# Layer 0's last tile in a two-layer graph network: GpSimd's additions behind VectorE's pieces, and two TensorE steps of the next stage a place earlier

## The chip, the cores and the metric

The kernel runs on one core of a Trainium2 chip. Its engines are TensorE (PE in the profile; its weight loads are shown as PEld), VectorE (DVE), ScalarE (ACT), GpSimd (POOL) and SyncE (SP), which issues most of the loads. The metric is the device time of one execution in microseconds (us), as the median of several runs. One further execution was taken by the hardware profiler; all times inside the kernel are from that one, counted from the start of its span.

## What is computed

Eight batches of 2048 nodes with 64 channels pass through two graph layers. Each adds its output to its input and normalises every node over its 64 channels.

```python
# layer 0: w = embedding x weight (D = 16, K = 3), per node
As = [eye(N), A, 2.0 * (A @ A) - eye(N)]
x_g = einsum('knm,bmc->bnkc', stack(As), x)
out = einsum('bnki,nkio->bno', x_g, w) + b
x = layernorm(x + out)
# layer 1: both supports are the same adj
out = concat([x, A x, 2 A A x - x, A x, 2 A A x - x]) @ weight + bias
x = layernorm(x + out)
```

The adjacency matrix is sparse, its rows are scaled by one number each, and the kernel works with its pattern of zeros and ones.

## The kernel before

The work is cut into 16 tiles of 128 nodes. The stages follow one another in program order: two hops of layer 0 (products with the 2048 x 2048 pattern); for each tile the mixing with the per-node weights (`mix0`), its norm and the projection for layer 1; then two hops of layer 1 and the output. TensorE is busy nearly throughout.

**Order.** Instructions that go through `ordered` (L127) stay in program order on their engine. So each of VectorE, ScalarE and GpSimd has one strict queue, and an instruction that waits holds back all behind it. SyncE's loads are in program order too (L123). Waits for data and buffers are put in by the framework, which also decides which of a ring's buffers a new tile gets.

**The pieces of a tile.** `mix0` (L402) has eight pieces, each a product into its own pair of PSUM banks; there are four pairs. A piece is (g, i): g is the half of the batches, 0 or 1. With i under 2, ScalarE scales the piece by the node's embedding and puts it aside in two SBUF tiles (L423, tiles `aside` of the ring `raw`, which has five buffers). With i of 2 or more, VectorE adds it into the sum `acc` by four instructions (L433). `add_aside(g)` then lets GpSimd add the aside tiles together, in three instructions, and the result into half g of `acc` by a fourth (all L441). The list `at[n]` says what is put into the program ahead of piece n.

**The norm.** `layernorm` (L359) is a generator. Its first part reduces `acc` (L362, L363, VectorE) and subtracts the mean on GpSimd (L365), giving `xc`; n1 squares on ScalarE (L353); n2 sums the squares (L370, VectorE) and takes the root (L372, ScalarE); n3 takes the reciprocal (L374, VectorE) and finishes with six GpSimd instructions (L375 to L380), the last of which multiplies `xc`. During tile t the norm of tile t-1 is finished.

**The last tile, 15.** Its `at` lists (L874 to L880) hold, besides n1 to n3 of tile 14's norm, the calls `early(i, ...)`: parts of step i of the next stage, namely the high part (ScalarE, L234) and low part (VectorE, L238) of the operand y, the load of S (L123) and its cast (ScalarE, L646). Steps 0 and 1 get all of them early, steps 2 to 4 only y. The pieces of the last tile are (0,0), (0,1), (0,4), (1,0), (0,5), (1,1), (1,4), (1,5).

**The next stage.** `third` is layer 1's first hop as seven products of eight steps each (`seven_products`, L580). A step is eight matmuls (L658). Its load of S has the lead 4, its cast of S the lead 2: they stand that many steps ahead in the program. S is loaded into the ring `raw`, where the aside tiles are, too. Its accumulators take over the four pairs of PSUM banks. In the first product the accumulators of the second, `sums3[1]`, are free, and there the last two tiles are finished: `last_transposed` transposes `xc` (eight on TensorE, L300, and ScalarE's copy hT, L306), `last_projected` projects it (sixteen matmuls, L460, and six ScalarE copies to z, L469). For tile 14 these come after steps 1 and 2, for tile 15 after steps 6 and 7 (L830 to L833). The norm of tile 15 is finished by three calls in the list `todo` (L892), of which two entries are taken after each step: n1 and n2 after step 2, n3 after step 3.

Of the kernel before, what the change touches and what calls it, by code (L numbers as in the profile page):

```python
# [14 lines left out]
ALU = mybir.AluOpType  # L15
# [5 lines left out]
NT = N // P  # L21
# [18 lines left out]
def pattern(  # L40
# [22 lines left out]
    nc = tc.nc  # L63

    def pool(stack, name, bufs, **kw):
        return stack.enter_context(tc.tile_pool(name=name, bufs=bufs, **kw))
# [17 lines left out]
    def bank(name):  # L84

        return psum.tile([P, 2, 512], F32, tag="ps", name=name)
# [20 lines left out]
    part = keep.tile([P, B], F32, tag="part", name="part")  # L107
# [19 lines left out]
    def ordered(ins):  # L127
        if in_order:
            tc.keep_in_program_order(ins)
# [28 lines left out]
    def keep_node_bias(pb, h):  # L158
        to = ebias[:, 8 * h : 8 * h + 8, :].rearrange("p (g t) c -> p g (t c)", g=2)
        ordered(nc.vector.tensor_copy(to, pb[h][:, :, : 4 * C]))  # L160
# [198 lines left out]
    def layernorm(src):  # L359

        s = work.tile([P, B], F32, tag="ln_s", name="s")
        ordered(nc.vector.tensor_reduce(s, src, AX.X, ALU.add))  # L362
        ordered(nc.vector.tensor_tensor(s, s, part, ALU.mult))  # L363
        xc = xcpool.tile([P, B, C], F32, tag="ln_xc", name="xc")
        ordered(nc.gpsimd.tensor_tensor(xc, src, wide(s), ALU.subtract))  # L365
        yield xc.rearrange("p b c -> p (b c)")
        sq = squares(xc)
        yield
        ss = work.tile([P, B], F32, tag="ln_ss", name="ss")
        ordered(nc.vector.tensor_reduce(ss, sq, AX.X, ALU.add))  # L370
        sd, r0, va, q, r = [work.tile([P, B], F32, tag=f"{name}{B}", name=name) for name in ("ln_sd", "ln_r0", "ln_v", "ln_q", "ln_r")]
        ordered(nc.scalar.activation(sd, ss, AF.Sqrt, bias=eps, scale=1.0 / C))  # L372
        yield
        ordered(nc.vector.reciprocal(r0, sd))  # L374
        ordered(nc.gpsimd.tensor_scalar(va, ss, -0.5 / C, -0.5 * EPS, ALU.mult, ALU.add))  # L375
        ordered(nc.gpsimd.tensor_tensor(q, r0, r0, ALU.mult))
        ordered(nc.gpsimd.tensor_tensor(q, q, va, ALU.mult))
        ordered(nc.gpsimd.tensor_scalar(q, q, 1.0, 1.5, ALU.mult, ALU.add))
        ordered(nc.gpsimd.tensor_tensor(r, q, r0, ALU.mult))
        ordered(nc.gpsimd.tensor_tensor(xc, xc, wide(r), ALU.mult))  # L380
        yield
# [20 lines left out]
    def mix0(t, tt, acc, at, pieces):  # L402

        def block(pm, lhsT, ds):
            for k in range(3):
                for n in range(3):
                    for j in range(2):
                        q = slice(j * C, (j + 1) * C)
                        nc.tensor.matmul(  # L409
                            pm[:, j], lhsT=tt[k][n][q, lhsT, :], rhs=w_parts[n][k][q, ds, :],  # L410
                            start=(k == 0 and n == 0), stop=(k == 2 and n == 2),
                        )

        def e(d):
            return emb_sb[:, t, d : d + 1]

        def by_batch(g, i):
            pm = bank("pm").rearrange("p j (d c) -> p j d c", c=C)
            block(pm, 2 * g + i, slice(0, 2 * DG))
            if i == 0:  # L420
                aside[g] = [rawp.tile([P, DG, 2, 2, C], F32, tag="raw", name="aside") for _ in range(2)]
            for d in range(2 * DG):
                ordered(nc.scalar.activation(aside[g][d // DG][:, d % DG, :, i, :], pm[:, :, d, :], AF.Copy, scale=e(d)))  # L423

        def by_four(g, dg):
            dg -= 2
            pm = bank("pm").rearrange("p j (i d c) -> p j i d c", i=2, d=DG)
            for i in range(2):
                block(pm[:, :, i], 2 * g + i, slice(dg * DG, (dg + 1) * DG))
            for d in range(DG):  # L430
                part = acc[:, 4 * g : 4 * g + 4, :]
                got = pm[:, :, :, d, :].rearrange("p j i c -> p (j i) c")
                ordered(nc.vector.scalar_tensor_tensor(part, got, e(dg * DG + d), part, ALU.mult, ALU.add))  # L433

        aside = {}

        def add_aside(g):
            one, other = [a.rearrange("p d j i c -> p d (j i) c") for a in aside[g]]
            part = acc[:, 4 * g : 4 * g + 4, :]
            for to, more in ((one, other), (one[:, :2], one[:, 2:]), (one[:, 0], one[:, 1]), (part, one[:, 0])):  # L440
                ordered(nc.gpsimd.tensor_tensor(to, to, more, ALU.add))  # L441

        for n, (g, i) in enumerate(pieces):
            for work_here in at[n]:
                if isinstance(work_here, int):
                    add_aside(work_here)
                else:
                    work_here()
            (by_batch if i < 2 else by_four)(g, i)
        return layernorm(acc)  # L450

    def project(t, hT, pus=None):
# [260 lines left out]
    pieces = chain(weights(), weight_parts())  # L713
# [38 lines left out]
    def piece():  # L752
        ordered(next(pieces))

    more = {
        (0, 3): [
            lambda: node_bias(sums2[1]),
            lambda: todo.extend(lambda h=h: keep_node_bias(sums2[1], h) for h in range(2)),
        ],
        1: [piece] * 11,  # L760
        (2, 0): [lambda: load_weights(0, 2)],
        (3, 0): [lambda: load_weights(1)],
        2: [piece] * 8,
# [21 lines left out]
    def last_transposed(t):  # L785
        last_h["T"] = transpose(last_h[t], "hT", sums3[1][0])

    def last_projected(t):
        project(t, last_h["T"], (sums3[1][1], sums3[1][0]))
        if t < NT - 1:  # L790
            return
        layer0.close()
        t_pool = pool(tpool, "fzT", 1, reuse_waits="tile")
        for a in range(2):
            for c in range(2):
                zT[a, c] = t_pool.tile([P, 4, B * C], F32, tag=f"zT{a}{c}", name="zT")
# [22 lines left out]
    def quarter_back(a, b, which):  # L819
# [9 lines left out]
    third = seven_products(0, to_zT, sums3, {  # L829
        (0, 1): [lambda: last_transposed(NT - 2)],  # L830
        (0, 2): [lambda: last_projected(NT - 2)],
        (0, 6): [lambda: last_transposed(NT - 1)],
        (0, 7): [lambda: last_projected(NT - 1)],  # L833
        **{(2 + t // KK, t % KK): [lambda t=t: add_bias(t)] for t in range(NT)},
        3: quarter_back(1, 1, 1), 4: quarter_back(0, 1, 0), 5: quarter_back(0, 0, 1),
    }, wait=2)
# [3 lines left out]
    def early(i, *kinds):  # L840

        got = third_got.setdefault(i, {})
        for lead, part in sorted(third[i], key=lambda part: -part[0]):
            if part.__name__ in kinds:
                part(got)
        third[i] = [part for part in third[i] if part[1].__name__ not in kinds]
# [4 lines left out]
    y, s = ("y_high", "y_low"), ("load_sum", "operands")  # L851
    acc, h, norm = first_tile[5], None, None
    tt = first_tile[0]
    coming = operands(1)
    for t in range(NT):
        got, last = {}, t == NT - 1
        at = [[] for _ in range(8)]
        n1, n2, n3 = [lambda: next(norm)] * 3 if t else [nothing] * 3

        if not last:  # L860
            following, of_x, of_hop, of_second = coming
            of_hop = of_hop()
            at[1] += [go(of_x)] * (1 if t else 3)
            at[2] += [go(of_hop), n1, go(of_hop), go(of_hop), n2]
            if t + 2 < NT:
                at[2] += [lambda: times_r(t + 2)]
                at[4] += [lambda: got.update(coming=operands(t + 2))]
            at[3] += [n3, go(of_second), lambda: got.update(acc=begin_sum(t + 1))]
            at[4] += [go(of_second), go(of_second)]
            at[6] += [0]  # L870
            at[7] += [lambda: got.update(hT=transpose(h, "hT"))] if t else []
            pieces = [(0, 0), (0, 4), (0, 5), (1, 2), (0, 1), (1, 3), (1, 4), (1, 5)]
        else:
            at[1] += [n1, lambda: early(0, *y, *s)]  # L874
            at[2] += [n2, n3, lambda: early(1, *y, *s)]
            at[3] += [0, lambda: early(2, *y)]
            at[4] += [lambda: early(3, *y)]
            at[5] += [lambda: early(4, *y)]
            at[7] += [1]
            pieces = [(0, 0), (0, 1), (0, 4), (1, 0), (0, 5), (1, 1), (1, 4), (1, 5)]  # L880
        norm_now = mix0(t, tt, acc, at, pieces)
        if 0 < t < NT - 1:
            project(t - 1, got["hT"])
        if "coming" in got:
            coming = got["coming"]
            next(coming[1])
            next(coming[1])
        norm = norm_now
        last_h[t] = h = next(norm)
        if not last:  # L890
            tt, acc = following, got["acc"]
# [480 lines left out]
```

## Time and profile before

| | |
|---|---|
| median of 3 runs | 765.86 us (765.76 to 765.98) |
| the profiled execution, whole | 768.08 us |
| its span in the profile | 766.3 us |
| mean granted clock of TensorE | 0.996 |
| busy: VectorE, ScalarE, GpSimd | 559.4, 407.1, 270.0 us |
| tile 15's pieces on TensorE | 508.67 to 525.86 us |
| first matmul of the next stage | 527.91 us |
| first matmul of its second product | 549.60 us |

Every line of a profile names the source line, the engine, the operation, and output and inputs by the program's names. A wait is written as who waited, an arrow, and who released it, followed by the sum, the number and the longest. The chain of work that ended last is followed back from the last instruction of the run, at each step to whatever released it. The table of stretches gives busy time and number of instructions for each engine, then the clock that TensorE was granted (1.00 is full speed), the DMA share and GB/s. "x4" after an operation means four instructions merged into one row, with the time from the first's start to the last's end.

### The profile page before, as it was taken

Reading aid. Unit: us, or ns where it says so; the run is one execution under the profiler, and the core shown is the slowest. Engines: PE = TensorE matmul, PEld = TensorE weight load, DVE = VectorE, ACT = ScalarE, POOL = GpSimd, SP = SyncE. Lnnn points to the kernel's source line nnn. Section 1 sums busy time; section 2 is a strip of 40 time slices with the busy share of each in tenths; the row PEclk is TensorE's granted clock in tenths of the full one; section 3 lists DMA queues with packets and bytes.
Section 4 is the critical chain, followed back from the end, with each engine's and each line's share of the span. In section 5 each row is a group of like instructions: output and inputs, shape, how many; then the busy total and the mean of one; then the engine's idle time right before and its main releaser. Section 6 shows DMA issues by size and latency. Waiting matters only on the chain.

```text
span 766.3 us, 16926 instructions
## 1 busy us (share of the span) xinstructions
PE 755.8 (99%) x6634; PEld 661.4 (86%) x6634; DVE 559.4 (73%) x1159; ACT 407.1 (53%) x896; POOL 270.0 (35%) x297
## 2 busy tenths in 40 slices
PE   9999999999999999999999999998999999999996
PEld 6888888888889999999999999997788888888885
DVE  6768867678748888888888888866588648668663
ACT  5456533878755555555555555565887663112111
POOL 0000000000026788777778888867100000011341
PEclk9999999999999999999999999999999999999999
DMA  9998996555511000000000000003354444565631
GB/s 323 371 388 269 348 317 212 173 169 160 171 56 31 16 16 15 17 16 15 17 16 16 15 17 2 2 30 97 104 168 142 137 152 137 176 182 171 212 126 45
DMA packets 73558, 96.69 MB, mean 126 GB/s; under 512 B 4864, under 2 KB 48384, under 8 KB 73344
## 3 DMA queue, kind: packets, MB, share of 16 engines
q1 hardware_dynamic: 62064, 76.66, 31.5%
q10 hardware_dynamic: 11408, 18.89, 6.6%
q8 instruction: 54, 0.88, 0.5%
q14 instruction: 32, 0.26, 0.1%
HBM read 76.65 MB, written 18.87 MB: 125 GB/s over the span
## 4 chain that ended last, share of the span: by engine, by line
PE 96%; ACT 2%; POOL 1%; DVE 1%; issue 0%; POOLq 0%; DVEq 0%
PE pm L409 34%; PE accT L658 27%; PE acc L254 15%; PE a L254 10%; PE accT L254 6%; PE pu L460 2%; PE pt L300 1%; PE first L143 1%; PE accT L810 1%; POOL aside L441 1%; ACT aside L423 1%; ACT z L469 0%; DVE acc L433 0%; ACT s L646 0%; PE accT L460 0%
## 5 line engine op out<-in xcount | busy, mean ns | idle before, releaser
L433 DVE SCALAR_TENSOR_TENSOR acc<-pm,pack_sb,acc 128x256 f32<-128x256 f32 x376 | 181.0, 482 | 43.8 <-PE pm L409 28.1
L658 PE MATMUL accT<-s,hl 128*128 128x512 f32 x896 | 208.1, 393 | 2.6 <-DVE acc L433 2.1
L409 PE MATMUL pm<-wh,hl 64*128 64x512 f32 (+1 forms) x1332 | 207.8, 303 | 0.0
L409 PE MATMUL pm<-wm,parts 64*128 64x512 f32 (+1 forms) x1332 | 203.4, 296 | 0.0
L409 PE MATMUL pm<-wl,parts 64*128 64x512 f32 (+1 forms) x1332 | 203.3, 296 | 0.0
L658 PEld LDWEIGHTS accT<-s,hl 128*128 128x128 f32 x896 | 168.4, 189 | 39.1 <-issue 2.5
L409 PEld LDWEIGHTS pm<-wh,hl 64*128 64x128 f32 x1332 | 130.8, 187 | 4.0 <-issue 0.4
L409 PEld LDWEIGHTS pm<-wl,parts 64*128 64x128 f32 x1332 | 130.7, 187 | 3.7
L409 PEld LDWEIGHTS pm<-wm,parts 64*128 64x128 f32 x1332 | 130.4, 187 | 3.8
L646 ACT CAST s<-raw 128x1024 fp32r<-128x1024 bf16 x104 | 109.8, 1056 | 40.7 <-ACT hl L234 23.8
L254 PE MATMUL acc<-hl,s 128*128 128x512 f32 x512 | 116.5, 390 | 0.0
L254 PEld LDWEIGHTS acc<-hl,s 128*128 128x128 f32 x512 | 96.0, 188 | 20.4 <-issue 0.3
L423 ACT ACTIVATE aside<-pm,pack_sb 128x128 f32<-128x128 f32 x272 | 74.2, 389 | 48.1 <-PE pm L409 48.1
L709 POOL TENSOR_TENSOR z<-z,rrow 128x512 f32<-128x512 f32 x16 | 21.0, 1314 | 212.1 <-DVE z L682 212.1
L234 ACT CAST hl<-z 128x256 fp32r<-128x256 f32 (+1 forms) x96 | 47.8, 517 | 59.7 <-PE acc L254 22.9
L441 POOL TENSOR_TENSOR aside<-aside 128x1024 f32<-128x1024 f32 (+2 forms) x51 | 75.4, 1478 | 2.7
L254 PE MATMUL a<-hl,s 128*128 128x512 f32 (+1 forms) x352 | 73.4, 370 | 0.0
L254 PEld LDWEIGHTS a<-hl,s 128*128 128x128 f32 x352 | 61.9, 188 | 11.3
L320 POOL TENSOR_TENSOR parts<-parts 128x512 fp32r<-128x512 f32 x45 | 58.4, 1298 | 34.9 <-DVE parts L314 27.4
L238 DVE TENSOR_TENSOR hl<-z,hl 128x512 fp32r<-128x512 f32 (+1 forms) x96 | 54.0, 568 | 16.8 <-ACT hl L234 13.8
L287 POOL TENSOR_TENSOR z<-z,got 128x512 f32<-128x512 f32 x3 | 4.8, 1622 | 142.6 <-ACT got L286 142.6
L254 PE MATMUL accT<-hl,s 128*128 128x512 f32 x192 | 44.3, 390 | 0.0
(136 smaller groups left out, 814.1 us busy)
## 6 DMA issues: line engine op xcount, KB each, us to landing
raw<-in_adj SPq DMA_DIRECT2D x58, 512.0 KB, 5.8
raw<-sums_of SPq DMA_DIRECT2D x64, 256.0 KB, 2.8
sums_of<-z ACTq DMA_DIRECT2D x16, 512.0 KB, 6.7
raw<-quarters SPq DMA_DIRECT2D x32, 256.0 KB, 2.7
raw<-in_adj SPq DMA_DIRECT2D x16, 384.0 KB, 3.4
quarters<-seen ACTq DMA_DIRECT2D x16, 256.0 KB, 6.2
xt<-in_xT SPq DMA_DIRECT2D x16, 256.0 KB, 2.7
z<-in_x SPq DMA_DIRECT2D x15, 256.0 KB, 6.9
```

Source lines behind the costliest of these rows:

```text
L234: ordered(nc.scalar.copy(to[0], src))
L238: ordered(nc.vector.tensor_tensor(to[1], src, to[0], ALU.subtract))
L254: nc.tensor.matmul(accs[i], lhsT=s[:, i * P : (i + 1) * P], rhs=hl[h], start=(first and h == 0), stop=(last and h == 1),)
L320: ordered(nc.gpsimd.tensor_tensor(mixed, mixed, low, ALU.add))
L409: nc.tensor.matmul(pm[:, j], lhsT=tt[k][n][q, lhsT, :], rhs=w_parts[n][k][q, ds, :], start=(k == 0 and n == 0), stop=(k == 2 and n == 2),)
L423: ordered(nc.scalar.activation(aside[g][d // DG][:, d % DG, :, i, :], pm[:, :, d, :], AF.Copy, scale=e(d)))
L433: ordered(nc.vector.scalar_tensor_tensor(part, got, e(dg * DG + d), part, ALU.mult, ALU.add))
L441: ordered(nc.gpsimd.tensor_tensor(to, to, more, ALU.add))
L460: nc.tensor.matmul(pm[:, j, i * 3 * C : (i + 1) * 3 * C], lhsT=hT[q, 2 * g + i, :], rhs=v[q], start=True, stop=True,)
L646: ordered(nc.scalar.copy(s, got["raw"]))
L658: nc.tensor.matmul(acc[i][:, c], lhsT=hl[h][:, i * P : (i + 1) * P], rhs=S[:, c * 512 : (c + 1) * 512], start=(kk == 0 and h == 0), stop=( ...
L709: ordered(nc.gpsimd.tensor_tensor(to, to, r, ALU.mult))
```

## The change

`add_aside` is split into `sum_aside`, the three additions among the aside tiles, and `add_aside`, the one into `acc`. In tiles 0 to 14 the two stand together where the whole stood. In the last tile:

- the addition of half 0 into `acc` moves from ahead of piece 3 to ahead of piece 6, behind VectorE's piece (0,5);
- the sums of half 1 stay ahead of piece 7, and their addition into `acc` moves behind piece 7, VectorE's (1,5), as a ninth place `at[8]`;
- n3 of tile 14's norm moves from ahead of piece 2 to ahead of piece 3, so behind VectorE's piece (0,4).

In the next stage, the transposes and the projection of tile 15 move from after steps 6 and 7 to after steps 5 and 6.

```diff
+        def sum_aside(g):
+            one, other = [a.rearrange("p d j i c -> p d (j i) c") for a in aside[g]]
+            for to, more in ((one, other), (one[:, :2], one[:, 2:]), (one[:, 0], one[:, 1])):
+                ordered(nc.gpsimd.tensor_tensor(to, to, more, ALU.add))
+
         def add_aside(g):
-            one, other = [a.rearrange("p d j i c -> p d (j i) c") for a in aside[g]]
             part = acc[:, 4 * g : 4 * g + 4, :]
-            for to, more in ((one, other), (one[:, :2], one[:, 2:]), (one[:, 0], one[:, 1]), (part, one[:, 0])):
-                ordered(nc.gpsimd.tensor_tensor(to, to, more, ALU.add))
-
-        for n, (g, i) in enumerate(pieces):
+            one = aside[g][0][:, 0].rearrange("p j i c -> p (j i) c")
+            ordered(nc.gpsimd.tensor_tensor(part, part, one, ALU.add))
+
+        for n, (g, i) in enumerate([*pieces, (None, None)]):
             for work_here in at[n]:
-                if isinstance(work_here, int):
-                    add_aside(work_here)
+                if isinstance(work_here, tuple):
+                    for part in work_here[0]:
+                        {"sum": sum_aside, "add": add_aside}[part](work_here[1])
                 else:
                     work_here()
-            (by_batch if i < 2 else by_four)(g, i)
+            if n < len(pieces):
+                (by_batch if i < 2 else by_four)(g, i)
...
-        (0, 6): [lambda: last_transposed(NT - 1)],
-        (0, 7): [lambda: last_projected(NT - 1)],
+        (0, 5): [lambda: last_transposed(NT - 1)],
+        (0, 6): [lambda: last_projected(NT - 1)],
...
-        at = [[] for _ in range(8)]
+        at = [[] for _ in range(9)]
...
-            at[6] += [0]
+            at[6] += [(("sum", "add"), 0)]
...
             at[1] += [n1, lambda: early(0, *y, *s)]
-            at[2] += [n2, n3, lambda: early(1, *y, *s)]
-            at[3] += [0, lambda: early(2, *y)]
+            at[2] += [n2, lambda: early(1, *y, *s)]
+            at[3] += [n3, (("sum",), 0), lambda: early(2, *y)]
             at[4] += [lambda: early(3, *y)]
             at[5] += [lambda: early(4, *y)]
-            at[7] += [1]
+            at[6] += [(("add",), 0)]
+            at[7] += [(("sum",), 1)]
+            at[8] += [(("add",), 1)]
```

## The prediction

> **What bounds the kernel.** I read the shares of the page first, then the waits of TensorE (PE), then the chain of work that ended last around the longest of them, then the granted clock and each engine's order of work there.
>
> ```profile
> PE 755.8 (99%) x6634; PEld 661.4 (86%) x6634; DVE 559.4 (73%) x1159; ACT 407.1 (53%) x896; POOL 270.0 (35%) x297
> ```
>
> PE is the bound, so an edit is worth only what it takes out of PE's idle or slowed time. Between the start and the last tile of layer 1 one wait matters (us in total, times, longest):
>
> ```profile
> PE accT L658 <- DVE acc L433: 2.1, 1, 2.1
> PE accT L658 <- ACT z L469: 0.4, 1, 0.4
> ```
>
> The chain (start, length) shows what it waited for:
>
> ```profile
> 517.34 0.21 DVE ln_r L374
> ...
> 519.05 1.05 POOL xc L380
> 520.10 2.55 POOL aside L441
> ...
> 524.96 0.74 POOL acc L441
> 525.70 0.03 issue
> 525.73 0.49 DVE acc L433
> ...
> 527.78 0.14 issue
> 527.91 5.50 PE accT L658 x16
> ```
>
> Tile 15's last matmul starts at 525.57 and could be followed at 525.70. The next bank holds piece (0,5), and VectorE (DVE) reads that piece only after POOL has added group 0's aside sums into acc (525.70). PE stands until 527.91. Then it is slow as well:
>
> ```profile
> 527.50:528.00 0.50, 0.09 (x1) 0.12 (x2) 0.50 (x2) 0.00 (x0) 0.50 (x1) 1.00 0.45 172
> 528.50:529.00 0.50, 0.50 (x2) 0.40 (x2) 0.47 (x2) 0.50 (x1) 0.50 (x1) 0.50 0.09 12
> 531.50:532.00 0.50, 0.50 (x3) 0.39 (x3) 0.46 (x2) 0.00 (x0) 0.00 (x0) 0.91 0.00 0
> ```
>
> The third column from the right is the granted clock: 0.50 from 528.2 to 531.6. Steps 0 and 1 took 5.44 us to the transposes at 533.35; steps 5 and 6 took 3.85 (541.38 to 545.23). The slow clock cost 1.59.
>
> Last, what may become late instead: DVE's and ScalarE's (ACT's) order of work, and SyncE's waits.
>
> ```profile
> 517.34 0.20 DVE L374 RECIPROCAL ln_r<-ln_sd 128x8 f32<-128x8 f32 x1 [2.19 <-ACT ln_sd L372]
> 517.98 2.04 DVE L433 SCALAR_TENSOR_TENSOR acc<-pm,pack_sb,acc 128x256 f32<-128x256 f32 x4
> 521.26 1.66 DVE L238 TENSOR_TENSOR hl<-z,hl 128x256 fp32r<-128x256 f32 x1 [0.88 <-ACT hl L234]
> 525.28 1.05 ACT L646 CAST s<-raw 128x1024 fp32r<-128x1024 bf16 x1 [1.51 <-DMA raw<-corner]
> 528.44 1.05 ACT L646 CAST s<-raw 128x1024 fp32r<-128x1024 bf16 x1 [1.81 <-DMA raw<-corner]
> SPq L123 <- POOL aside L441: 11.5, 1, 11.5
> ```
>
> The loads of S for steps 2, 3, 4 and 5 leave at 522.66, 525.72, about 528.3 and 531.14: each as POOL lets go of an aside buffer of the same five-buffer ring. **POOL's pace paces the loads**, and the casts follow 2.62 and 2.72 us after the issue.
>
> [...] the 0.42 us subtraction at 521.26 took 1.66 because POOL's first addition ran to 522.64; the additions that read PSUM kept 0.49 beside POOL. [...]
>
> **The change, part by part.**
>
> *Piece (0,5) before POOL's addition.* No instruction is added; the single POOL addition into acc goes behind DVE's four. In tile 14 DVE's (1,5) at 507.72 didn't wait for POOL's addition into the other half of acc at 509.58, so halves are tracked apart, and (1,4) and (1,5) won't wait for it. PE finishes (0,5) at 519.4. DVE reaches it after the subtraction of step 3 (521.26 + 0.34), so it runs 521.6 to 523.7[...] **Removed: 2.21 of standing and 1.59 of slow clock.** The same cover leaves (1,4) at 525.5 to 527.5 (a subtraction ahead of it waits for POOL until 525.2), (1,5) to 529.5, just by the transposes' need at 529.5.
>
> *The norm's root (L374 to L380) behind piece (0,4).* One DVE reciprocal and POOL's last five norm instructions (L376 to L380) move behind four DVE additions; POOL's L375, which needs no root, is early anyway. DVE gains nothing: (0,4) stood behind the step-1 subtraction, which needs ACT's cast (517.6) anyhow. The reciprocal goes from 517.34 to 519.93, and POOL's queue with it, by 2.59: xc of tile 14 is done at 522.69 (was 520.10; needed at 529.5, free), the first addition at 525.23, the sum at 527.47, the addition into acc at 528.29. Group 1 follows: first addition 528.29 + 2.55 = 530.84; all 528.29 + 5.35 = **533.64** (5.35 is 525.70 to 531.12 without its 0.15 wait on DVE, plus an issue gap). Before it was 531.12, but DVE's (1,5) followed and ended at 533.21; now (1,5) is long done. So the reduction L362 starts at 533.67 instead of 533.23, and the subtraction of the mean ends at 535.78 (2.11 after the addition, as in tile 14: 510.33 to 512.44).
>
> *The loads behind POOL.* Step 2: issue 525.25, cast at 527.87. Step 3: issue 528.31, cast 531.03 to 532.0. Step 4: issue 530.86, cast 533.56. If step 3 gets the buffer that PE frees at 525.7 instead, its cast is at 529.2; which one is not in the trace. I take the later: in the run before no early issue shows that buffer used.
>
> *PE from 525.70*, with 1.84 a step, 0.17 more ahead of a transpose or projection, 0.39 for eight transposes, 1.50 for a projection (all from its starts before):
> - steps 0 and 1, transposes of tile 14 at 529.5, step 2 at 529.9, projection wanted at 531.95. ACT copies hT behind step 3's cast (532.0 + 0.59), so 532.65: **0.70 lost**.
> - Steps 3, 4 to 537.83. Step 5's cast stands on ACT behind z's six copies (from 534.51, behind step 4's cast), the squares (536.1) and the root. Copies to end of that cast took 4.57 before (536.75 to 541.32), so 539.08; step 5 at 539.14: **1.31 lost**. Before, 0.42 was lost there.
> - *Transposes and projection of tile 15 a step earlier* (eight transposes and ACT's hT copy; sixteen matmuls and six ACT copies). They come after step 5, at 541.15. The xc of tile 15: sums of squares at 536.82, reciprocal 1.73 later (539.06 to 540.79 before), xc 2.99 after that: 541.54. **0.45 lost**; before, xc (543.78) was ready for 545.23.
> - Step 6 at 542.0, projection 544.04, step 7 at 545.54, step 8 at **547.38**. The six copies (544.8 to 546.5) lie beside step 7; before, step 8 waited 0.44 for them. On ACT they pass two high parts and two casts, of steps 8 and 9; the latter ends near 547.7, wanted at 549.2. SP's loads and DVE aren't passed. The pool closed with the projection has no instruction of its own on PE.
>
> Removed 2.21 + 1.59 + 0.42 + 0.44 = 4.66; added 0.70 + 1.31 + 0.45 = 2.46. **Gain 2.2**, as 549.60 - 547.38 says. From 549.60 PE runs to the end without a listed wait, so the gain is kept. The profiled execution (768.08, span 766.3) would become 765.9 (span 764.1); on the median, 765.86 - 2.2 = **763.65**.
>
> **Rivals.**
> - *The clock drops again* (0.20). [...] a throttle costs 1.59 again: gain 0.6, **765.25**, no measurable change. [...]
> - *The refilled chain is shorter* (0.14): step 3's load takes PE's buffer, or ACT and POOL gain half of the new gaps: gain 3.4, **762.4**. With no new gap it would be 761.2, but POOL's 5.35 of sums speaks against.
> - *The earlier transposes wait for xc* (0.12, slower). They sit at the head of PE's queue. [...] step 8 at 551.3, **767.6**. Break-even is xc at 543.8. Against: in the run before that POOL stretch (541.07 to 543.78) was only 0.24 longer than in tile 14.
> - That it doesn't do what it says (POOL's addition still ahead of (0,5)) I exclude: both engines keep program order.
>
> **Numbers.** Forecast 0.54 (762.9 to 764.4 by itself), so faster by over 0.2% has 0.68, within 0.2% 0.20, slower 0.12; 0.2% (1.5 us) is about what a measurement tells from none. The range runs from 762.4, the shorter chain, to 765.4, the second throttle; what lies outside is the slower case and the tail below.
>
> **What would show it.** No PE wait on L433 at 525.7 and a clock of 1.00 at 528 to 532: first step right. POOL's addition into acc near 528.3 and L362 near 533.7: second. PE waits for hT at 532, for s at 539, for xc at 541.2: third. No wait on L469 ahead of step 8: fourth. Wrong if the clock shows 0.50 after 532, or if step 8 isn't near 547.4.

## The result, and the profile after

| | before | changed |
|---|---|---|
| median | 766.24 us (22 runs, 765.76 to 768.82) | 765.36 us (22 runs, 764.87 to 766.26) |
| the profiled execution, whole | 768.08 us | 765.98 us |
| its span | 766.3 us | 764.2 us |

The ratio is 0.9986 (95% interval 0.998 to 0.9993): about 1.1 us faster, 0.5 to 1.5 by the interval. The forecast was 2.2 us faster, 763.65; 765.36 lies just inside the far end of the range. The profiled spans moved by 2.1, close to the forecast, but the medians by 0.9. That gap is the main subject of what follows.

The busy times of the changed kernel, first as on its page:

```profile
PE 754.5 (99%) x6634; PEld 658.8 (86%) x6634; DVE 559.0 (73%) x1159; ACT 407.4 (53%) x896; POOL 269.6 (35%) x297
```

PE's waits in the changed kernel (us in total, times, longest), without one of 1.3 us at the start of the run that both kernels have. L664 is the old L658, L466 the old L460, L652 the old L646, L475 the old L469. L440 are GpSimd's sums of aside tiles and L445 its addition into `acc`, both L441 before:

```profile
PE accT L664 <- ACT s L652: 0.8, 1, 0.8
PE accT L300 <- POOL xc L380: 0.3, 1, 0.3
PE accT L466 <- ACT hT L306: 0.2, 1, 0.2
```

The two waits of before, on VectorE's L433 and on the copies to z, are gone. The three that the prediction named are there. The granted clock (third column from the right) where it was 0.50 before:

```profile
528.00:529.00 1.00, 1.00 (x6) 0.84 (x5) 0.93 (x3) 0.90 (x1) 1.00 (x2) 1.00 0.00 0
530.00:531.00 1.00, 1.00 (x12) 0.81 (x12) 0.00 (x0) 0.00 (x0) 0.92 (x2) 1.00 0.42 160
```

Where PE waits, the chain of work that ended last now runs over POOL, a load of S (`raw<-corner`) and ACT:

```profile
527.67 0.74 POOL acc L445
528.42 2.36 POOL aside L440
530.79 2.60 DMA raw<-corner
533.39 0.02 issue
533.42 1.05 ACT s L652
534.46 1.64 ACT z L475 x6
536.11 0.54 ACT sq L353
...
540.16 1.23 POOL xc L380
541.39 0.04 issue
541.44 0.46 PE accT L300 x8
```

And VectorE's order in the changed kernel:

```profile
518.37 2.04 DVE L433 SCALAR_TENSOR_TENSOR acc<-pm,pack_sb,acc 128x256 f32<-128x256 f32 x4
520.32 0.20 DVE L374 RECIPROCAL ln_r<-ln_sd 128x8 f32<-128x8 f32 x1
...
522.00 2.04 DVE L433 SCALAR_TENSOR_TENSOR acc<-pm,pack_sb,acc 128x256 f32<-128x256 f32 x4
523.95 1.69 DVE L238 TENSOR_TENSOR hl<-z,hl 128x256 fp32r<-128x256 f32 x1
525.56 4.18 DVE L433 SCALAR_TENSOR_TENSOR acc<-pm,pack_sb,acc 128x256 f32<-128x256 f32 x8
533.79 0.69 DVE L362 TENSOR_REDUCE s<-acc 128x8 f32<-128x512 f32 x1 [4.05 <-POOL acc L445]
```

Piece (0,5) runs at 522.00 to 524.04 and no longer waits for GpSimd; the subtraction behind it takes 1.69 in place of 0.42, beside POOL's first addition (to 525.36); the tile's norm waits for GpSimd until 533.79.

To compare executions whose tile 15 begins at different times, I use one **stretch**: from tile 15's first matmul to the first transposes back (L810 before, L816 in the changed kernel), both starts as the chain lists them. Before: 600.67 - 508.98 = 91.69. Changed: 598.26 - 509.38 = 88.88, so 2.81 less. Ahead of the stretch the changed run took 0.4 longer, behind it 0.3, so that its span is only 2.1 shorter: that this is nearly the forecast is chance.

### The profile page after: what moved, and what is told of

The parts are those of the page before. It is cut to its first block, busy times and chain, and to the rows that moved or that the text cites. A ratio compares the mean times of both kernels' runs of the same rounds, so it can differ in the third digit from the quotient of the medians.

```text
span 764.2 us, 16926 instructions
## 1 busy us (share of the span) xinstructions
PE 754.5 (99%) x6634; PEld 658.8 (86%) x6634; DVE 559.0 (73%) x1159; ACT 407.4 (53%) x896; POOL 269.6 (35%) x297
## 4 chain that ended last, share of the span: by engine, by line
PE 95%; POOL 2%; ACT 1%; DVE 1%; DMA 0%; issue 0%; POOLq 0%; DVEq 0%
PE pm L409 34%; PE accT L664 25%; PE acc L254 15%; PE a L254 10%; PE accT L254 6%; PE pu L466 2%; PE pt L300 1%; POOL aside L440 1%; PE first L143 1%; PE accT L816 1%; ACT aside L423 1%; DMA raw<-corner 0%; POOL xc L380 0%; ACT s L652 0%; DVE acc L433 0%; ACT z L475 0%
## 5 line engine op out<-in xcount | busy, mean ns | idle before, releaser
L433 DVE SCALAR_TENSOR_TENSOR acc<-pm,pack_sb,acc 128x256 f32<-128x256 f32 x376 | 181.1, 482 | 40.1 <-PE pm L409 28.1
L664 PE MATMUL accT<-s,hl 128*128 128x512 f32 x896 | 206.6, 391 | 0.8 <-ACT s L652 0.8
L409 PE MATMUL pm<-wh,hl 64*128 64x512 f32 (+1 forms) x1332 | 204.1, 303 | 0.0
L409 PE MATMUL pm<-wm,parts 64*128 64x512 f32 (+1 forms) x1332 | 199.7, 296 | 0.0
L409 PE MATMUL pm<-wl,parts 64*128 64x512 f32 (+1 forms) x1332 | 199.6, 296 | 0.0
L664 PEld LDWEIGHTS accT<-s,hl 128*128 128x128 f32 x896 | 167.3, 188 | 36.7 <-ACT s L652 1.2
L652 ACT CAST s<-raw 128x1024 fp32r<-128x1024 bf16 x104 | 110.0, 1058 | 43.4 <-ACT hl L234 23.4
L409 PEld LDWEIGHTS pm<-wh,hl 64*128 64x128 f32 x1332 | 126.8, 187 | 4.6 <-issue 0.4
L409 PEld LDWEIGHTS pm<-wl,parts 64*128 64x128 f32 x1332 | 126.7, 187 | 4.3
L409 PEld LDWEIGHTS pm<-wm,parts 64*128 64x128 f32 x1332 | 126.4, 187 | 4.4
L440 POOL TENSOR_TENSOR aside<-aside 128x1024 f32<-128x1024 f32 (+2 forms) x51 | 75.1, 1473 | 2.7
```

Of the source, the lines that this page charges most:

```text
L409: nc.tensor.matmul(pm[:, j], lhsT=tt[k][n][q, lhsT, :], rhs=w_parts[n][k][q, ds, :], start=(k == 0 and n == 0), stop=(k == 2 and n == 2),)
L652: ordered(nc.scalar.copy(s, got["raw"]))
L664: nc.tensor.matmul(acc[i][:, c], lhsT=hl[h][:, i * P : (i + 1) * P], rhs=S[:, c * 512 : (c + 1) * 512], start=(kk == 0 and h == 0), stop=( ...
```

## The experiments

Two questions: which part of the change does what, and why the medians show less than half of what the two profiles show. Theory A says that the slow clock was in few executions of before, so removing it isn't in the median. Theory B says that it was in nearly all, and that the changed kernel loses the gain elsewhere.

### The idle time filled with work

```diff
             for i in range(2):
-                block(pm[:, :, i], 2 * g + i, slice(dg * DG, (dg + 1) * DG))
+                for _ in range(2 if t == NT - 1 and g == 1 and dg == 3 else 1):
+                    block(pm[:, :, i], 2 * g + i, slice(dg * DG, (dg + 1) * DG))
```

> The kernel before, with the product of tile 15's last piece, (1,5), computed twice into the same bank (the second writes the same values again), 36 matmuls or 2.15 us more on PE. They fill the 2.2 us in which PE stood, so that PE goes on at 527.9 as before, but without an idle stretch and so without a slow clock. Theory A (the clock drop of 1.59 us fell in the one profiled execution of before and in few others): the median stays within 0.4 us of before, and the longest runs of before (over 767) have no counterpart. Theory B (the drop falls in nearly every execution of before): about 1.6 us faster, ratio 0.998.

Measured: 766.71 us, ratio 1.0009 (1.0001 to 1.0017): not faster, but 0.56 slower by the medians, a little more than theory A allowed. PE has no wait at the start of the next stage, the clock is 1.00 there, and the stretch is 90.18. Theory B's 1.6 us isn't there. The 2.15 us of work cost more than the stand that they fill, 0.44 by the stretch of the next run (89.74) and 0.56 by the medians, so the usual stand is nearer 1.7 than 2.2. The absence of long runs says nothing here, because the runs of before beside it had none either (at most 767.06).

### Before once more

> The kernel before once more, unchanged. Theory A (the profiled execution of before was one of few with the drop, and with VectorE's subtraction of step 2 ahead of GpSimd's first addition it also stood 0.3 to 0.5 us longer than usual): no stretch at 0.50 before the end of the output, PE's wait on L433 is 1.7 to 2.1, and the stretch from tile 15's first matmul to the first transposes back is 89.7 to 90.2 in place of 91.7. Theory B: 0.50 for one window again, stretch near 91.7. The median is that of before within 0.3 us under both.

No edit. Measured: 766.57 us, ratio 1.0003 (0.9993 to 1.0012). Its profiled execution took 766.14 us. PE's waits, then VectorE's order, then the clock:

```profile
PE accT L658 <- DVE acc L433: 1.7, 1, 1.7
PE accT L658 <- ACT z L469: 0.4, 1, 0.4
```

```profile
519.63 3.97 DVE L238 TENSOR_TENSOR hl<-z,hl 128x256 fp32r<-128x256 f32 x2
525.04 2.04 DVE L433 SCALAR_TENSOR_TENSOR acc<-pm,pack_sb,acc 128x256 f32<-128x256 f32 x4 [1.44 <-POOL acc L441]
```

```profile
528.00:529.00 1.00, 1.00 (x6) 0.83 (x5) 0.93 (x3) 0.76 (x1) 0.92 (x2) 1.00 0.54 123
```

The stretch is 598.38 - 508.64 = **89.74**, 1.95 less than in the execution that the prediction read, with the clock at 1.00 and a stand 0.35 shorter by the listed wait. Against this one the changed kernel's 88.88 is 0.86 better, and the medians differ by 0.88. Of the 22 runs, the 8 with 768.27 us or more have a mean granted clock of 0.996, as the first profile had; the other 14 (767.15 or less) have 0.997 to 0.999. No run of the changed kernel shows 0.996. So **theory A holds**: by the mean clock, the drop is in some executions of the unchanged kernel. They are more on this chip, with 7 of another 27 runs of before, than on the two other chips of these experiments, with 4 of 33 and none of 51. None is among the changed one's 22. Where before has the drop, the change saves about 3 us (768.27 or more in the 8 long runs, a median of 765.36 in the changed kernel); the median of before hardly shows that.

The shorter stand comes from GpSimd, whose addition into half 0 was done 16.38 us after the start of the stretch here and 16.72 in the first profile. VectorE and GpSimd in the first profile:

```profile
517.63 0.49 POOL L376 TENSOR_TENSOR ln_q<-ln_r 128x8 f32<-128x8 f32 x1 [2.19 <-DVE ln_r L374]
519.93 0.45 DVE L238 TENSOR_TENSOR hl<-z,hl 128x256 fp32r<-128x256 f32 x1
520.05 4.83 POOL L441 TENSOR_TENSOR aside<-aside 128x1024 f32<-128x1024 f32 x3
```

GpSimd here:

```profile
517.28 0.20 POOL L376 TENSOR_TENSOR ln_q<-ln_r 128x8 f32<-128x8 f32 x1 [2.19 <-DVE ln_r L374]
519.47 4.72 POOL L441 TENSOR_TENSOR aside<-aside 128x1024 f32<-128x1024 f32 x3
```

In the first profile GpSimd's first small operation (L376) started together with step 1's subtraction (517.63) and took 0.49; here it began just ahead of that and took 0.20. Then step 2's subtraction began before GpSimd's first addition, which took 2.55 in the chain; here GpSimd was first (2.38), and the two subtractions took 3.97 for both. So in both meetings an operation took longer where one of the other engine was already under way or started with it; no run tests the first of the two by itself.

### Each part alone

The root alone, on the kernel before:

```diff
-            at[2] += [n2, n3, lambda: early(1, *y, *s)]
-            at[3] += [0, lambda: early(2, *y)]
+            at[2] += [n2, lambda: early(1, *y, *s)]
+            at[3] += [n3, 0, lambda: early(2, *y)]
```

> The kernel before with only the norm's root moved behind piece (0,4). Measure: the stretch from tile 15's first matmul to the first transposes back (L810); before 91.7 us with the slow clock and 90.1 without. GpSimd's addition into the sum comes some 2.3 us later, and with it VectorE's (0,5) and the next stage: PE stands 4.5 instead of 2.2. Theory A [...] every execution now has the drop: stretch 94, all runs 3.5 to 4 us slower than before. Theory B (2.2 us always triggers it): only 2.3 us slower than before.

Measured: 770.77 us (770.15 to 772.43), ratio 1.0056 (1.0042 to 1.007), stretch 94.88. First PE's row at the start of the next stage, then two stretches of time at the edges of the slow clock:

```profile
530.73 0.76 PE L658 MATMUL accT<-s,hl 128*128 128x512 f32 x1 [4.26 <-DVE acc L433]
```

```profile
529.00:530.00 1.00, 0.00 (x0) 0.00 (x0) 0.93 (x3) 0.63 (x2) 1.00 (x1) 0.72 0.42 100
536.00:536.50 0.50, 0.50 (x3) 0.46 (x2) 0.47 (x2) 0.00 (x0) 0.00 (x0) 0.74 0.95 356
```

All five runs are at least 3.88 us above the median of before, as theory A says; the median is 4.5 above, more than its 3.5 to 4. In the profiled execution the clock is at 0.50 for 6.8 us instead of 3.4, so it costs more than my 1.59: steps 0 and 1 took 6.47 us where they take 3.87 at full clock. That execution is the slowest of the five, 1.66 above their median. Three of the other four have the same mean clock of 0.994; the fastest has 0.996, so it spent less time at half clock.

The transposes and projection alone, on the kernel before:

```diff
-        (0, 6): [lambda: last_transposed(NT - 1)],
-        (0, 7): [lambda: last_projected(NT - 1)],
+        (0, 5): [lambda: last_transposed(NT - 1)],
+        (0, 6): [lambda: last_projected(NT - 1)],
```

> Only the last part: transposes and projection of tile 15 after steps 5 and 6, the rest as before. xc of tile 15 comes at 543.8 and step 5 ends at 543.4, so PE waits 0.4 there and saves 0.44 ahead of step 8: within 0.3 us of before under both theories. The slower rival would show as 1 us or more slower.

Measured: 766.19 us, ratio 0.9999 (0.999 to 1.0007), stretch 89.70 against 89.74: nothing, as expected. PE's wait for the copies to z (0.4) is replaced by one for xc (0.3). The clock stays at 1.00 although PE waits 1.7 here too.

The additions alone: the changed kernel with the root early and the two steps where they were.

```diff
-            at[2] += [n2, lambda: early(1, *y, *s)]
-            at[3] += [n3, (("sum",), 0), lambda: early(2, *y)]
+            at[2] += [n2, n3, lambda: early(1, *y, *s)]
+            at[3] += [(("sum",), 0), lambda: early(2, *y)]
...
-        (0, 5): [lambda: last_transposed(NT - 1)],
-        (0, 6): [lambda: last_projected(NT - 1)],
+        (0, 6): [lambda: last_transposed(NT - 1)],
+        (0, 7): [lambda: last_projected(NT - 1)],
```

> Only the first part of the change: GpSimd's additions into the sum behind VectorE's pieces; root early and transposes and projection of tile 15 after steps 6 and 7 as before. Against the run with the root early it should lose the 0.44 us that step 8 waits for the copies to z: 2.6 to 3.1 us faster than before under theory A, about 4.2 under theory B. If the earlier transposes were harmful (my slower rival), it would be the faster of the two.

Measured: 764.71 us, ratio 0.9981 (0.9973 to 0.9988), stretch 88.21. In the stretch it is faster than the whole change, but by 0.67 and not by 1.6 or more; the intervals of the two ratios overlap. Against the second profile of before the additions alone take 1.53 out of the stretch, and 1.44 by the medians. So they give the whole gain, and the other two parts together take 0.67 of it back.

### The root early

Only the first hunk of the last diff, so additions and steps are moved, the root not.

> The changed kernel with the norm's root (n3) put back ahead of piece 2; the other two parts stay. My account says that moving the root cost POOL 2.59 us and through it all three new waits of PE (2.46 us forecast): they go, and step 8 of the next stage follows tile 15's start by some 2.4 us less than in the changed kernel. Theory A: 1.0 (the change as measured) plus 2.4, so 3.0 to 3.5 us faster than before, ratio 0.9955 to 0.996. Theory B: 4.5, ratio 0.994. Rival (the root's place is what makes the rest work, since (0,5) then comes later on VectorE, held by GpSimd's first addition): no faster than the changed kernel, and PE waits for L433 at the start of the next stage.

Measured: 764.78 us, ratio 0.9981 (0.9974 to 0.9988), stretch 88.22: 0.66 better than the changed kernel, not 2.4. It equals the additions alone (88.21), so the earlier steps change nothing here either; the 0.44 that I expected from them isn't there, since a wait for xc (0.3) replaces the one for the copies to z (0.4). What costs 0.66 in the changed kernel is the root's move. VectorE, then GpSimd, then PE's waits:

```profile
520.04 3.96 DVE L238 TENSOR_TENSOR hl<-z,hl 128x256 fp32r<-128x256 f32 x2
523.93 2.03 DVE L433 SCALAR_TENSOR_TENSOR acc<-pm,pack_sb,acc 128x256 f32<-128x256 f32 x4
```

```profile
519.88 4.72 POOL L440 TENSOR_TENSOR aside<-aside 128x1024 f32<-128x1024 f32 x3
526.10 0.79 POOL L445 TENSOR_TENSOR acc<-acc,aside 128x256 f32<-128x256 f32 x1 [1.50 <-DVE acc L433]
```

```profile
PE accT L300 <- POOL xc L380: 0.3, 1, 0.3
PE accT L664 <- DVE acc L433: 0.2, 1, 0.2
```

The rival that I had written down is half right. With the root early, GpSimd's long additions fall on the two subtractions, (0,5) comes 2 us later, PE waits 0.2 for it, and GpSimd itself waits 1.5 for VectorE. So the norm of tile 15 (L362) starts only 1.17 us earlier than in the changed kernel (23.24 against 24.41 after the start of the stretch). The late root avoids that; my account had charged it 2.59 us and credited nothing.

### The two subtractions behind the piece

On the kernel with the root early:

```diff
-            at[3] += [(("sum",), 0), lambda: early(2, *y)]
-            at[4] += [lambda: early(3, *y)]
-            at[5] += [lambda: early(4, *y)]
+            at[3] += [(("sum",), 0), lambda: early(2, "y_high")]
+            at[4] += [lambda: early(3, "y_high")]
+            at[5] += [lambda: early(2, "y_low"), lambda: early(3, "y_low"), lambda: early(4, *y)]
```

> Root early, and the subtractions of steps 2 and 3 (L238) moved behind VectorE's piece (0,5). [...] in the run with the root early these two waited in turn for GpSimd's first and second additions (3.96 us for both) and put (0,5) at 523.9 to 526.0, 15 us after the tile's start, which made PE wait 0.2 and GpSimd's addition into the sum 1.5. Behind (0,5) they hold nothing up: (0,5) runs at 520.1, the addition follows the sums without a wait, xc of tile 15 comes 0.5 to 1.5 earlier, and the stretch is 87.6 to 88.0 (88.2 with the root early). Rival [...]: nothing changes.

Measured: 764.26 us, ratio 0.9973 (0.9962 to 0.9985), stretch 88.00: faster than before, and below the changed kernel's 88.88. It is 0.22 below the run with the root early, too little for the times to tell. VectorE and GpSimd:

```profile
518.47 4.18 DVE L433 SCALAR_TENSOR_TENSOR acc<-pm,pack_sb,acc 128x256 f32<-128x256 f32 x8
522.57 2.73 DVE L238 TENSOR_TENSOR hl<-z,hl 128x256 fp32r<-128x256 f32 x3
```

```profile
520.26 4.75 POOL L440 TENSOR_TENSOR aside<-aside 128x1024 f32<-128x1024 f32 x3
525.09 0.81 POOL L445 TENSOR_TENSOR acc<-acc,aside 128x256 f32<-128x256 f32 x1
```

Pieces (0,4) and (0,5), eight additions that read PSUM, ran straight through GpSimd's multiplication of xc and its first addition at their usual 0.5 us each. The three subtractions, both of whose inputs are in SBUF, took 2.73 where three times 0.42 is usual, but now little stood behind them. GpSimd's wait of 1.5 and PE's of 0.2 are gone, as expected; in the rival nothing would have changed. The forecast for the end was too good: L362 starts 1.36 earlier than with the root early, but xc of tile 15 comes only 0.22 earlier, not 0.5 to 1.5. The next runs show why.

### Loads of their own

On the changed kernel:

```diff
-                got["raw"] = rawp.tile([P, 2, Q], BF16, tag="raw", name="raw")
+                where, tag = (work2, "t0") if s == 0 and p == 0 and kk in (2, 3) else (rawp, "raw")
+                got["raw"] = where.tile([P, 2, Q], BF16, tag=tag, name="raw")
```

> The changed kernel with S of steps 2 and 3 loaded into two buffers that are free at that time (those of tag t0), not into the ring of the aside tiles. My account says that GpSimd's pace holds these loads and, through ScalarE's queue, hT and the copies to z. Then the casts of steps 2 and 3 come at 525 to 527, PE's wait for hT (0.2) goes, and of the wait for step 5's cast (0.8) only what the norm of tile 15 needs is left: stretch 88.4 to 88.7 against 88.9 of the changed kernel. Rival (the loads aren't on the path; the norm alone is): 88.9.

Measured: 765.27 us, ratio 0.9986 (0.998 to 0.9993), stretch 88.85: as the changed kernel. The rival is right. The casts of steps 2 and 3 came at 524.8 and 526.1, the wait for hT went, and the wait for step 5's cast grew from 0.8 to 1.0. What held ACT is seen in its order (its squares are L353):

```profile
532.67 1.75 ACT L475 COPY z<-accT 128x256 f32<-128x256 f32 x6 [1.05 <-PE accT L466]
535.18 0.63 ACT L353 ACTIVATE sq<-xc 128x512 f32<-128x512 f32 x1 [0.76 <-POOL xc L365]
```

The copies to z are early, and the squares wait for GpSimd's xc. The chain through the load, which the profile names, and the chain through the norm end within 0.3 us of each other (in the changed kernel the copies at 536.11 and xc at 535.92); removing one moves nothing.

### Both together

Subtractions behind (0,5) with the root early, and the loads' own buffers.

> Both together: root early, subtractions of steps 2 and 3 behind (0,5), and their S in buffers of their own. If the two paths (loads, norm) each hold PE, both together give the most: stretch 87.2 to 87.6, and 0.5 us or more faster than the run with the root early (764.8 us median there), so 2.0 to 2.5 us faster than before.

Measured: 764.59 us, ratio 0.9974 (0.9965 to 0.9983), stretch 87.97: no better than the subtractions alone, and 0.4 to 0.8 short of what I expected in the stretch. ACT again:

```profile
532.64 1.75 ACT L475 COPY z<-accT 128x256 f32<-128x256 f32 x6 [1.05 <-PE accT L466]
534.23 0.69 ACT L353 ACTIVATE sq<-xc 128x512 f32<-128x512 f32 x1
```

Now the copies wait for PE's own projection, and the squares stand behind them in ACT's queue, though xc was there (since 532.79). A third chain, which starts on PE, holds tile 15's norm. Moving the squares ahead of the copies wasn't tried.

## Why the prediction was right or wrong

| step of the prediction (us) | forecast | changed kernel |
|---|---|---|
| stand at the start of the next stage | gone | gone |
| xc of tile 14, from tile 15's start | 13.71 | 13.60 |
| GpSimd's addition into half 0 done | 19.31 | 19.03 |
| norm's first reduction (L362) starts | 24.69 | 24.41 |
| lost for hT | 0.70 | 0.33 |
| lost for step 5's cast | 1.31 | 1.05 |
| lost for xc of tile 15 | 0.45 | 0.44 |
| lost for the copies to z | 0 | 0 |

(The losses are counted from the starts of the steps, as in the prediction: the projection was due at 532.43 and started at 532.76, step 5 due at 537.94 and started at 538.99, the transposes at 541.00 and 541.44.)

**Right: the mechanism.** Each removed wait went, each new one came where it was forecast. What replaced the stand is a chain over GpSimd and ACT, and more than half of the removed standing came back there.

**Right: that the earlier steps do no harm.** The slower rival, PE held by the earlier transposes, didn't occur: alone and beside the additions they changed nothing. The 0.44 that was counted for them as removed came back as the wait for xc, which the sum had at 0.45.

**Wrong: "Removed: 2.21 of standing and 1.59 of slow clock".** Both terms were read from one execution, which wasn't typical. The table ahead of the prediction had the warning: the profiled execution took 768.08 us and the median was 765.86. The prediction read what was removed in the one and took it off the other as well. The second profile of the unchanged kernel has no drop and a wait of 1.7 instead of 2.1. Counted from starts as before, its stand is 1.88, and 0.41 and 0.45 are lost ahead of steps 5 and 8: 2.74 to be removed, not 4.66.

**Mis-sized: the new waits, 2.46 against 1.82.** GpSimd was 0.28 us faster to L362 than I took it: 0.11 by the end of xc (the norm's first small operation took 0.27 here and 0.49 in the profile that I had read, but the multiplication 1.18 in place of 1.05), and 0.17 in the additions, of which the first took 2.38 in place of 2.55. So the working should have been 2.74 - 1.82 = 0.92; 0.86 is the difference of the two stretches, 0.88 that of the medians. That 765.36 still lies inside the range is luck: its upper end of 765.4 was set for a second drop of the clock, which isn't what happened.

**Wrong inside a right sum: "the loads behind POOL".** They are late, and the chain names them, but with early loads the time is the same. **And the root's move** isn't a plain cost of 2.59: put back, it gives 0.66 in the stretch and not 2.4, since the late root also keeps GpSimd's long additions off VectorE's subtractions.

The rival in which the clock drops in the new gaps did not occur in the profiled execution (1.00 until PE's work ends), and none of the 22 runs has the 0.996 of the long runs of before: those with 0.997 are among the fastest, too. The four executions of before that I had were not alike: the three at 765.76 to 765.98 most likely had no drop, and only the profiled one had it.

What stays open: whether every execution with the drop also has the longer stand. It is likely, as those runs were 2 us and more above the median of the others and the drop alone costs 1.6, but only one of them was profiled.

## What to carry to other kernels

Before pricing anything in a profile, compare the profiled execution's own time with the median: where it is 2 us above, look for what in it may not be in the others, above all a slow clock, and leave it out of the gain. When a wait is moved off one engine, follow each queue to the next two chains that end within half a microsecond, since removing the named one alone gave nothing here (the loads' own buffers). And an instruction placed early on VectorE "for free" isn't free beside long GpSimd additions: with the root early, two subtractions of 0.42 us with both inputs in SBUF took 3.96 together and put piece (0,5) 2 us later. Place such ones where nothing waits behind them.

## What the runs showed of the hardware

- A stand of PE of 2.06 us, by its wait for L433 (until 527.91), was followed by a drop of the clock: in the first profile of before it went to 0.50 at 528.2. With a stand of 1.72 us in the second profile of before, and of 1.71 in the run of the steps alone, it stayed at 1.00, and steps 0 and 1 took 3.89 us in both by the chain, against 5.50 with the drop. These are one execution each; how long a stand it takes isn't shown.
- The drop lasted 3.4 us in the first profile of before (528.2 to 531.6), with PE busy throughout it. With the root alone, where PE stood for 4.26 us, it lasted 6.8 (529.44 to 536.3): PE stood for the first 1.3 us of it, until 530.73, and was busy for the other 5.5. Why it lasted twice as long there isn't shown.
- Tenths of a microsecond decide which of VectorE and GpSimd goes first: the same program ran step 2's subtraction 0.12 us ahead of GpSimd's first addition in one execution (it took 0.45) and 0.16 behind it in another (it and the next subtraction took 3.97 together).
